# Attention and a nonlocal block on one core: reciprocals of the softmax sums kept as one row per unit, and three pieces of the last image's work moved forward

## The chip, the cores and the metric

The kernel runs on one core of a Trainium2 chip, in float32. The metric is the device time of one execution in microseconds; less is better. The work is done by the core's engines side by side: TensorE (PE) multiplies matrices, VectorE (DVE) and ScalarE (ACT) do elementwise work, GpSimd (POOL) a little of it, and SyncE (SP) issues most of the transfers (DMA) between the DRAM and the on-chip memory. Each engine works through its own instructions in the order in which they stand in its program, and waits on semaphores for the others.

## The reference

There are 8 images of 512 channels and 32 x 32 = 1024 positions. Two layers follow each other:

```python
# layer 0: attention over the positions, 8 heads of 64 channels, with a residual
q, k, v = conv1x1(x, Wq, bq), conv1x1(x, Wk, bk), conv1x1(x, Wv, bv)      # (B, 8, 64, 1024)
attn = softmax(einsum('bhdn,bhdm->bhnm', q, k) * 64**-0.5, axis=-1)
x1 = x + conv1x1(einsum('bhnm,bhdm->bhdn', attn, v), Wp, bp)
# layer 1: a nonlocal block without softmax, 256 inner channels, then a norm over the batch
g, theta, phi = conv1x1(x1, g_w, g_b), conv1x1(x1, theta_w, theta_b), conv1x1(x1, phi_w, phi_b)
f = einsum('bcn,bdn->bcd', theta, phi) / 1024
z = conv1x1(einsum('bcd,bdn->bcn', f, g), W_w, W_b) + x1
out = (z - mean(z)) * rsqrt(var(z) + 1e-5) * gamma + beta                # over images and positions
```

## The kernel before, in words

**Products.** A 1x1 convolution is a matrix product of 512 (or 256) channels with the 1024 positions. `seven` forms it from seven products of quarter blocks instead of eight (the scheme of Strassen and Winograd): VectorE forms four sums of the data's quarters (`data_sums`, `more_sums`; t1 = 12 - 11, t2 = 22 - t1, t3 = 22 - 12, t4 = 21 - t2), TensorE forms the seven products in four PSUM banks, and the results are added up in SBUF by VectorE, the first of each quarter mostly by ScalarE. In some products two of the seven are split once more (`nested`; tiles with `_in_` in their names: `pk_in_s` and so on), which needs one more VectorE addition for each small product. The order of the TensorE instructions, and of those of VectorE and SyncE that are wrapped in `dve(...)` and `sp(...)`, is kept as it is written; the others are placed by a scheduler.

**Attention of one image** (`attention`). There are 4 pairs of heads and 2 halves of the queries: 8 units `u`, each of 8 blocks of keys `m`, 64 steps in all. A step is eight TensorE instructions for the scores `ps` (L423), an exponential on ScalarE (`e`, L426), an addition on VectorE into `acc` (L432), and, two steps later, eight TensorE instructions for `po` with v (L449). `acc` of a unit is 128 key rows x 2 heads x 512 queries, to be summed over the key rows. For that, `spread` (L459) sends it by four transfers to 32 partitions of the tile `fold`, so that four units stand beneath each other: units 0 to 3 are group 0, units 4 to 7 group 1. Three VectorE additions (L478) and one product with a matrix of ones (`columns`, tile `den`, L396) finish the sums, in a form in which every unit and head has 16 equal rows. `denominators` takes the reciprocal of all 128 rows on VectorE (L486) and writes them to the DRAM (`den_d`, L488). `normalize` reads one row of each sixteen back, sent to 64 partitions each (tile `r`, L497, four transfers of 512 KB), and multiplies `o`, the attention's result, by `r` in four VectorE instructions (L503). The buffer of `r` is that of `fold`: it can only be filled when `fold` has been read.

**The order of the stages.** While image b ends its attention, the sums for image b + 1 begin, and its q, v and k products (`pq`, `pv`, `pk`) stand between the attention of image b and its projection `pp`; `denominators` comes after `pq`, the products o*r come near the end of `pv`. Then follow `pp` with Wp (which makes x1), `ptp` (theta and phi; tile `tp`), `pg` (g), `pf` (f), `pwf` (f joined to W_w) and `pz` (z). In the last image, b = 7, there is no next image to stand in between. Instead the nonlocal block of image 6 was held back: its `pf` runs inside the attention of image 7, and its `pg`, `pwf` and first `pz` stand between the attention and the projection of image 7. For it the sums of image 6's x1 are formed once more (tiles `t_x_6_again`, shown as `t_x_again`, L202), from `near_end` (L746): in the last image `near_end` is called by the last step, forms t1 and t2, then calls `spread` for the last unit (the argument `midway` of `more_sums`), then forms t3 and t4. The reciprocals of group 0 are done at step 46 there, those of group 1 between the products of `pg`:

```python
nonlocal_(b - 1, held["x"], nxt["data"], held["f"], weights("WgT"), lambda: None,
          {3: lambda: nxt.update(d=denominators(next_bank(f"den_{b}_1")[:, 0, :]))})
z[b - 1] = [held["x"][:, cc, :] for cc in range(CC)]
between = {4: late_unit(b - 1, 0)}
normalize(nxt["d"])()
```

`theta_phi` (L536) forms the sums t3 and t4 of x1 after its first product. `put_away` (L638) writes g and wf of an image to the DRAM for the end; the last stage (`last_z`) finishes z of three images and writes all eight.

Of the kernel before, what the change touches and what calls it, by code (L numbers as in the profile page):

```python
# [8 lines left out]
F32 = mybir.dt.float32  # L9
# [7 lines left out]
P = 128  # L17
# [13 lines left out]
def unshifted(ctx: ExitStack, tc: tile.TileContext, a: dict, out: bass.AP):  # L31
    nc = tc.nc
    B, C, H, W = a["x"].shape
    N = H * W
    CC = C // P
    NB = N // P
    NH = N // 512
    D = C // HEADS
# [3 lines left out]
    IC = CI // P  # L42
# [23 lines left out]
    dve = sp = pe  # L66
# [123 lines left out]
    def data_sums(quarters, name, which=(1, 2, 3, 4), **how):  # L190

        data = dict(zip(("11", "12", "21", "22"), quarters), name=name)
        more_sums(data, which, **how)
        return data

    def more_sums(data, which, pin=lambda ins: None, midway=lambda: None):
        for i in which:
            l, r = {1: ("12", "11"), 2: ("22", "t1"), 3: ("22", "12"), 4: ("21", "t2")}[i]
            if i == 3:
                midway()  # L200
            data[f"t{i}"] = block(f"t{i}_{data['name']}")
            pin(nc.vector.tensor_tensor(data[f"t{i}"], data[l], data[r], ALU.subtract))  # L202

# [11 lines left out]
    def quarters_of(t):  # L215
        return [t[:, k * CC // 2:(k + 1) * CC // 2, h * 512:(h + 1) * 512] for k in range(2) for h in range(NH)]
# [91 lines left out]
    for x_part, w_part in (((0, 1, 0), (w_first[:, 0], 0, 0, 0, 1)), ((1, 2, 0), (w_first[:, 0], 0, 0, 1, 2)),  # L308
                           ((2, 4, 0), (w_first[:, 1], 0, 1, 0, 2)), ((0, 2, 1), (w_first[:, 2], 1, 1, 0, 2)),
                           ((2, 4, 1), (corner["WqT"], 1, 0, 0, 2))):  # L310
        c0, c1, h = x_part
# [86 lines left out]
    def attention(b, q, k, v, near_end, make_f=None):  # L398

        units = [(p, h) for p in range(NPAIR) for h in range(NH)]
        steps = [(u, m) for u in range(len(units)) for m in range(NB)]
        es, accs, sums, folded, o = {}, {}, {}, {}, {}
        tags = list(free)

        def part(u):
            p, h = units[u]
            return o["o"][:, p, h * 512:(h + 1) * 512]

        def scores(i):
            u, m = steps[i]
            p, h = units[u]
            ps = bank(tags[(0, 1, 3)[i] if i < 3 else (i + 1) % 2], f"ps_{b}_{u}_{m}")
            for j in range(2):
                r = slice(j * D, (j + 1) * D)  # L420
                for c in range(2):
                    keys = slice(m * P + c * P // 2, m * P + (c + 1) * P // 2)
                    pe(nc.tensor.matmul(ps[c * P // 2:(c + 1) * P // 2, j, :], k[r, p, keys],  # L423
                                        q[r, p, h * 512:(h + 1) * 512], start=True, stop=True, skip_group_check=True))
            e = block(f"e_{b}_{u}_{m}")
            nc.scalar.activation(e, ps, AF.Exp, scale=SCALE)  # L426
            es[u, m] = e
            if m == 1:
                accs[u] = w3.tile([P, 2, 512], F32, tag="acc", name=f"acc_{b}_{u}")
                nc.vector.tensor_tensor(accs[u], es[u, 0], e, ALU.add)  # L430
            elif m > 1:
                ins = nc.vector.tensor_tensor(accs[u], accs[u], e, ALU.add)  # L432
                if i == len(steps) - 1 and not make_f:
                    dve(ins)
            if m == NB - 1 and u == len(units) - 1 and make_f:
                near_end(lambda: spread(u, dve))
            elif m == NB - 1:
                spread(u)

        def weighted(i):  # L440
            u, m = steps[i]
            p, _ = units[u]
            if m == 0:
                sums[u] = bank(tags[2 + u % 2], f"po_{b}_{u}")
            ps, e = sums[u], es.pop((u, m))
            for r in range(2):
                keys = slice(r * P // 2, (r + 1) * P // 2)
                for j in range(2):
                    pe(nc.tensor.matmul(ps[j * D:(j + 1) * D, r, :], v[keys, m, (2 * p + j) * D:(2 * p + j + 1) * D],  # L449
                                        e[keys, j, :], start=(m == 0), stop=(m == NB - 1), skip_group_check=True))  # L450
            if m == NB - 1:
                if not o:
                    o["o"] = mats.tile([P, CC, N], F32, tag="o", name=f"o_{b}")
                nc.scalar.copy(part(u), ps[:, 0, :])
                ins = nc.vector.tensor_tensor(part(u), part(u), ps[:, 1, :], ALU.add)
                if i == len(steps) - 1 and not make_f:
                    dve(ins)

        def spread(u, pin=lambda ins: None):  # L459

            g, i = divmod(u, 4)
            if i == 0:
                folded[g] = foldp.tile([P, 4, 1024], F32, tag="fold", name=f"fold_{b}_{g}")
            acc = accs.pop(u).rearrange("p j n -> p (j n)")
            for k in range(4):
                eng = nc.scalar if make_f and u == len(units) - 1 and k % 2 else nc.sync
                eng.dma_start(folded[g][i * P // 4:(i + 1) * P // 4, k, :], acc[k * P // 4:(k + 1) * P // 4, :])
            if i == 3:
                t = folded[g]
                if g == 1 and not make_f:  # L470
                    return
                if g == 0:
                    folded[g] = fold1.tile([P, 1, 1024], F32, tag="fold1", name=f"fold1_{b}")
                for part_of in fold_parts(g, t, pin):
                    part_of()

        def fold_parts(g, t, pin):
            return [lambda to=to, l=l, r=r: pin(nc.vector.tensor_tensor(to, l, r, ALU.add)) for to, l, r in (  # L478
                (t[:, 0], t[:, 0], t[:, 1]), (t[:, 2], t[:, 2], t[:, 3]), (folded[g][:, 0], t[:, 0], t[:, 2]))]

        def denominators(g, ps):

            t = folded.pop(g)
            columns(ps, folds, lambda j: t[:, 0, j * 512:(j + 1) * 512])
            ri = t[:, 0, :512]
            nc.vector.reciprocal(ri, ps)  # L486
            d = dram2.tile([P, 512], F32, tag="den", name=f"den_d_{b}_{g}")
            nc.sync.dma_start(d, ri)  # L488
            return d

        def normalize(d):

            r = foldp.tile([P, 8, 512], F32, tag="fold", name=f"r_{b}")
            for g in range(2):
                for j in range(2):
                    rows_of = d[g].rearrange("(j i s) n -> j s i n", j=2, i=4)[j, 0]
                    sp(nc.sync.dma_start(r[j * D:(j + 1) * D, 4 * g:4 * g + 4, :], rows_of.partition_broadcast(D)))  # L497

            def products():
                for h in range(NH):  # L500
                    for g in range(2):
                        at = o["o"][:, 2 * g:2 * g + 2, h * 512:(h + 1) * 512]
                        dve(nc.vector.tensor_tensor(at, at, r[:, 4 * g + h:4 * g + 4:2, :], ALU.mult))  # L503

            return products

        for i in range(len(steps) + LAG):
            if i < len(steps):
                scores(i)
            if make_f and i == 2:  # L510
                make_f(bank(tags[2], f"pf_{b - 1}"))
            if not make_f and i == len(steps) - 2:
                near_end()
            if i >= LAG:
                weighted(i - LAG)
            if make_f and i == 46:
                first_den = denominators(0, bank(tags[2], f"den_{b}_0")[:, 0, :])
        free[:] = tags
        if make_f:
            return o["o"], lambda ps: denominators(1, ps), lambda d: normalize((first_den, d)), None  # L520
        return o["o"], denominators, normalize, fold_parts(1, folded[1], dve)
# [14 lines left out]
    def theta_phi(b, w, data, between):  # L536
# [8 lines left out]
        def first(q, ps):  # L545
            ins = nc.vector.tensor_tensor(at(q), as_tp(ps), tpb[:, int(q[0]) - 1].to_broadcast([P, NB // 2, CI]),
                                          ALU.add)
            if q == "11":
# [1 line left out]

        seven(f"ptp_{b}", w, data, True, first,
              lambda q, ps: nc.vector.tensor_tensor(at(q), at(q), as_tp(ps), ALU.add),
              {0: lambda: more_sums(data, (3, 4), pin=dve), **between})
        return tp

    def make_f(b, tp, ps):
# [81 lines left out]
    def put_away(b):  # L638

        xt, g, wf = late[b]  # L640
        for d in range(IC):
            nc.sync.dma_start(spill_g[b][:, d * N:(d + 1) * N], g[d])
        nc.sync.dma_start(spill_g[b][:, IC * N:], wf)

    def take_back(b):
        t = wr.tile([P, IC * N + IC * C], F32, tag="w", name=f"gwf_{b}")
# [93 lines left out]
    for b in range(B):  # L740
# [2 lines left out]
        if not last:  # L743
            nxt["x"] = load_x(b + 1)

        def near_end(midway=None):  # L746
            if last:
                nxt["data"] = data_sums(quarters_of(held["x"]), f"x1_{b - 1}_again", pin=dve, midway=midway)
            else:
                nxt["data"] = data_sums(quarters_of(nxt["x"]), f"x_{b + 1}", (1, 2))  # L750

        def held_f(ps):
            held["f"] = make_f(b - 1, held["tp"], ps)
# [40 lines left out]
        if b == B - LATE:  # L794
            for cc in range(CC):
                nc.sync.dma_start(spill[b][:, cc, :], xt[:, cc, :])
        data = data_sums(quarters_of(xt), f"x1_{b}", (1, 2))
        if last:
            reload_chunks(B - LATE)
        elif b > B - LATE and b != B - 2:  # L800
# [241 lines left out]
```

## Time and profile before

| | |
|---|---|
| time, median of 3 runs | 2181.84 us (2181.07 to 2182.1) |
| span of the profiled execution | 2180.1 us, 29638 instructions |
| TensorE busy | 2142.0 us, 98% of the span |
| VectorE busy | 1423.3 us, 65% |
| ScalarE busy | 741.5 us, 34% |
| DMA, mean over the span | 102 GB/s |
| `pp` of image 1 to `pp` of image 2 (530.47 to 795.83 in the chain of waits) | 265.4 us |
| r, 32 transfers of 512 KB, median from issue to landing | 9.8 us |

The profile names each instruction by its line, its engine, and the tiles that it writes and reads (`out<-in`). "Busy" is the time in which an engine had work in it; the waits are the idle stretches in front of an instruction, put down to what ended them. A wait put down to "issue" is one for which the profile shows no releaser. The chain of waits follows the execution back from its last instruction; where an engine's work runs without a break, the chain stays on it.

### The profile page before, as it was taken

What the parts mean: (1) busy time and instruction counts of PE and PEld (TensorE: products, weight loads), DVE (VectorE), ACT (ScalarE), POOL (GpSimd) and SP (SyncE); (2) the same over time, 40 slices, a digit from 0 to 9 for tenths busy, and PEclk for the clock granted to TensorE, in tenths of its full rate; (3) what the DMA queues carried; (4) which work ended last, traced back from release to release, by engine and by line L of the source; (5) the groups of instructions that cost most, each with busy time, mean ns of one, the idle gap of its engine ahead of it and who ended that gap; (6) DMA issues with size and microseconds to landing.
All of it is one profiled execution on the core that took longest, in us unless ns stands there. A gap on an engine that the chain in (4) does not pass through costs nothing.

```text
span 2180.1 us, 29638 instructions
## 1 busy us (share of the span) xinstructions
PE 2142.0 (98%) x12454; PEld 1109.4 (51%) x12454; DVE 1423.3 (65%) x1612; ACT 741.5 (34%) x848; POOL 45.1 (2%) x50
## 2 busy tenths in 40 slices
PE   9999999999999999999999999999999999999896
PEld 4534663356733566336563366533665346733362
DVE  6477656776477764777747767467673777568626
ACT  1463104631046310562106621165203641065015
POOL 0000100000000000000000000000000000000000
PEclk9999999999999999999999999999999999999998
DMA  6312433124131232313323132231424115111739
GB/s 215 133 38 62 127 150 130 40 66 118 68 131 40 77 108 101 108 40 84 99 93 107 40 103 97 111 81 39 132 99 153 40 30 158 57 40 39 262 127 358
DMA packets 58893, 223.40 MB, mean 102 GB/s; under 512 B 9344, under 2 KB 15744, under 8 KB 53248
## 3 DMA queue, kind: packets, MB, share of 16 engines
q1 hardware_dynamic: 57264, 220.11, 31.8%
q8 instruction: 100, 1.64, 0.3%
q10 hardware_dynamic: 1488, 1.32, 0.2%
q14 instruction: 41, 0.34, 0.0%
HBM read 138.03 MB, written 49.81 MB: 86 GB/s over the span
## 4 chain that ended last, share of the span: by engine, by line
PE 93%; DMA 2%; DVE 2%; issue 1%; ACT 1%; SPq 0%; DVEq 0%
PE ps L423 20%; PE po L449 20%; PE ptp L276 9%; PE pp L276 7%; PE pv L276 7%; PE pq L276 6%; PE pk L276 6%; PE pg L276 4%; PE pf L561 3%; PE pz L276 2%; PE pk_in_s L239 2%; PE pq_in_s L239 2%; PE pp_in_s L239 2%; PE pz L671 2%; DMA r<-den_d 1%; PE pwf L596 1%
## 5 line engine op out<-in xcount | busy, mean ns | idle before, releaser
L426 ACT ACTIVATE e<-ps 128x1024 f32<-128x1024 f32 x512 | 522.9, 1025 | 427.9 <-PE ps L423 422.4
L432 DVE TENSOR_TENSOR acc<-acc,e 128x1024 f32<-128x1024 f32 x384 | 470.0, 1224 | 129.3 <-ACT e L426 121.6
L449 PE MATMUL po<-e,v 64*64 64x512 f32 x4096 | 528.7, 589 | 0.7 <-ACT w_WgT L563 0.7
L423 PE MATMUL ps<-q,k 64*64 64x512 f32 x4096 | 529.1, 589 | 0.0
L449 PEld LDWEIGHTS po<-e,v 64*64 64x64 f32 x4096 | 156.5, 133 | 283.4 <-issue 275.4
L423 PEld LDWEIGHTS ps<-q,k 64*64 64x64 f32 x4096 | 155.6, 133 | 284.1 <-issue 275.0
L584 ACT ACTIVATE g<-pg,gb 128x512 f32<-128x512 f32 x31 | 21.3, 687 | 398.8 <-PE pg L276 395.9
L430 DVE TENSOR_TENSOR acc<-e,e 128x1024 f32<-128x1024 f32 x64 | 78.2, 1222 | 108.7 <-ACT e L426 73.4
L276 PE MATMUL ptp<-w_tp,t_x 128*128 128x256 f32 x512 | 116.7, 384 | 2.4 <-DVE t_x L202 2.4
L276 PE MATMUL pv<-w_WvT,t_x 128*128 128x256 f32 x512 | 114.5, 379 | 0.0
L276 PEld LDWEIGHTS ptp<-w_tp,t_x 128*128 128x128 f32 x512 | 97.8, 192 | 16.1 <-DVE t_x L202 2.9
L276 PEld LDWEIGHTS pv<-w_WvT,t_x 128*128 128x128 f32 x512 | 97.2, 190 | 13.2
L276 PE MATMUL pp<-t_o,w_WpT 128*128 128x512 f32 x208 | 100.9, 592 | 0.0
L276 PE MATMUL pq<-t_x,w_WqT 128*128 128x512 f32 x200 | 98.8, 593 | 0.9 <-DVE w_WqT L723 0.9
L276 PE MATMUL pk<-t_x,w_WkT 128*128 128x512 f32 x200 | 98.9, 592 | 0.0
L379 ACT COPY v<-pv 128x1024 f32<-128x1024 f32 x32 | 32.4, 1012 | 191.2 <-PE pv L276 191.2
L276 PE MATMUL pv<-w_WvT,x 128*128 128x256 f32 x384 | 87.5, 381 | 0.0
L276 PE MATMUL ptp<-w_tp,x 128*128 128x256 f32 x384 | 86.8, 379 | 0.0
L380 DVE TENSOR_TENSOR v<-v,pv 128x1024 f32<-128x1024 f32 x24 | 29.3, 1222 | 79.9 <-PE pv L276 79.9
L276 PEld LDWEIGHTS pv<-w_WvT,x 128*128 128x128 f32 x384 | 72.4, 190 | 15.7 <-issue 5.9
L276 PEld LDWEIGHTS ptp<-w_tp,x 128*128 128x128 f32 x384 | 73.0, 190 | 13.3 <-issue 3.6
L276 PE MATMUL pp<-o,w_WpT 128*128 128x512 f32 x144 | 70.1, 611 | 7.8 <-issue 5.2
(181 smaller groups left out, 2200.4 us busy)
## 6 DMA issues: line engine op xcount, KB each, us to landing
fold<-acc SPq DMA_DIRECT2D x254, 128.0 KB, 2.3
r<-den_d SPq DMA_DIRECT2D x32, 512.0 KB, 9.8
x<-in_x_dram SPq DMA_DIRECT2D x31, 512.0 KB, 6.1
w_WqT<-kept_WqT SPq DMA_DIRECT2D x7, 2176.0 KB, 8.8
w_WkT<-kept_WkT SPq DMA_DIRECT2D x7, 2176.0 KB, 8.3
w_WpT<-kept_WpT SPq DMA_DIRECT2D x6, 2176.0 KB, 8.9
w_WvT<-kept_WvT SPq DMA_DIRECT2D x7, 1792.0 KB, 7.2
w_tp<-kept_tp SPq DMA_DIRECT2D x7, 1792.0 KB, 7.4
```

Of the source, the lines that this page charges most:

```text
L239: pe(nc.tensor.matmul(ps, a[wi], d[di], start=s not in begun, stop=True, skip_group_check=True))
L276: pe(nc.tensor.matmul(to_ps, lhsT(k), rhs(k), start=(s, at) not in begun, stop=(k == nk - 1), skip_group_check=True))
L379: seven(f"pv_{b}", w, data, True, lambda q, ps: nc.scalar.copy(at(q), as_v(ps)), lambda q, ps: dve(nc.vector.tensor_tensor(at(q), at(q), a ...
L380: lambda q, ps: dve(nc.vector.tensor_tensor(at(q), at(q), as_v(ps), ALU.add)), between)
L423: pe(nc.tensor.matmul(ps[c * P // 2:(c + 1) * P // 2, j, :], k[r, p, keys], q[r, p, h * 512:(h + 1) * 512], start=True, stop=True, skip_gr ...
L426: nc.scalar.activation(e, ps, AF.Exp, scale=SCALE)
L430: nc.vector.tensor_tensor(accs[u], es[u, 0], e, ALU.add)
L432: ins = nc.vector.tensor_tensor(accs[u], accs[u], e, ALU.add)
L449: pe(nc.tensor.matmul(ps[j * D:(j + 1) * D, r, :], v[keys, m, (2 * p + j) * D:(2 * p + j + 1) * D], e[keys, j, :], start=(m == 0), stop=(m ...
L561: pe(nc.tensor.matmul(ps[:, c, :], tp[:, i, c * P:(c + 1) * P], tp[:, i, CI:], start=(i == 0), stop=(i == NB - 1)))
L596: pe(nc.tensor.matmul(ps, f[:, c, d * P:(d + 1) * P], ww[:, c, :], start=(c == 0), stop=(c == IC - 1)))
L671: pe(nc.tensor.matmul(ps[:, h - h0, :], wf[:, d, oc * P:(oc + 1) * P], g[d][:, h * 512:(h + 1) * 512], start=(d == 0), stop=(d == IC - 1), ...
```

## The change

What the change does, in the order of the diff:

- The reciprocals are written as one row for each unit and head: 8 rows of 512 (16 KB) in place of 128 rows (256 KB). `rows_of` then reads the four rows of one group and head as one run of 8 KB for each of 64 partitions, where before it was four runs of 2 KB.
- In the last image, the reciprocal of group 1 goes to a small tile of its own (`ri`), so that `fold` is free, and `r` can be filled, as soon as the product `den` has read it. The rows of group 0 are then loaded at once, ahead of group 1's reciprocal.
- The products o*r are done group by group instead of half by half.
- In the last image, `near_end` is called three times: t1 of image 6's x1 after step 59, t2 after step 61, and t3 and t4 at the end, after the last unit's transfers have been issued and ahead of the additions of the folding.
- `theta_phi` finds t3 and t4 of x1 done in the last image, ahead of its first product.
- The writes of image 6's g and wf are kept in their written order on SyncE, behind the loads of r.

```diff
-    def more_sums(data, which, pin=lambda ins: None, midway=lambda: None):
+    def more_sums(data, which, pin=lambda ins: None):
         for i in which:
             l, r = {1: ("12", "11"), 2: ("22", "t1"), 3: ("22", "12"), 4: ("21", "t2")}[i]
-            if i == 3:
-                midway()
...
             if m == NB - 1 and u == len(units) - 1 and make_f:
-                near_end(lambda: spread(u, dve))
+                spread(u, dve, near_end)
...
-        def spread(u, pin=lambda ins: None):
+        def spread(u, pin=lambda ins: None, meanwhile=lambda: None):
...
             if i == 3:
                 t = folded[g]
+                meanwhile()
                 if g == 1 and not make_f:
                     return
...
-            ri = t[:, 0, :512]
+            alone = make_f and g == 1
+            ri = (fold1.tile([P, 1, 1024], F32, tag="fold1", name=f"ri_{b}") if alone else t)[:, 0, :512]
             nc.vector.reciprocal(ri, ps)
-            d = dram2.tile([P, 512], F32, tag="den", name=f"den_d_{b}_{g}")
-            nc.sync.dma_start(d, ri)
+            if alone:
+                rows_of(0, first_den)
+            d = dram2.tile([8, 512], F32, tag=f"den{g}", name=f"den_d_{b}_{g}")
+            nc.sync.dma_start(d, ri.rearrange("(a s) n -> a s n", a=8)[:, 0, :])
             return d
 
+        def rows_of(g, d):
+            if "all" not in rows:
+                rows["all"] = foldp.tile([P, 8, 512], F32, tag="fold", name=f"r_{b}")
+            rows[g] = rows["all"][:, 4 * g:4 * g + 4, :].rearrange("q i n -> q (i n)")
+            for j in range(2):
+                sp(nc.sync.dma_start(rows[g][j * D:(j + 1) * D, :],
+                                     d.rearrange("(j i) n -> j (i n)", j=2)[j].partition_broadcast(D)))
+
         def normalize(d):
-            r = foldp.tile([P, 8, 512], F32, tag="fold", name=f"r_{b}")
             for g in range(2):
-                for j in range(2):
-                    rows_of = d[g].rearrange("(j i s) n -> j s i n", j=2, i=4)[j, 0]
-                    sp(nc.sync.dma_start(r[j * D:(j + 1) * D, 4 * g:4 * g + 4, :], rows_of.partition_broadcast(D)))
+                if g not in rows:
+                    rows_of(g, d[g])
+            r = rows["all"]
 
             def products():
-                for h in range(NH):
-                    for g in range(2):
+                for g in range(2):
+                    for h in range(NH):
                         at = o["o"][:, 2 * g:2 * g + 2, h * 512:(h + 1) * 512]
                         dve(nc.vector.tensor_tensor(at, at, r[:, 4 * g + h:4 * g + 4:2, :], ALU.mult))
...
-            if not make_f and i == len(steps) - 2:
+            if i in ((len(steps) - 5, len(steps) - 3) if make_f else (len(steps) - 2,)):
                 near_end()
...
-              {0: lambda: more_sums(data, (3, 4), pin=dve), **between})
+              {0: lambda: "t3" in data or more_sums(data, (3, 4), pin=dve), **between})
...
+        spill_dma = sp if b == B - 2 else lambda ins: None
         for d in range(IC):
-            nc.sync.dma_start(spill_g[b][:, d * N:(d + 1) * N], g[d])
-        nc.sync.dma_start(spill_g[b][:, IC * N:], wf)
+            spill_dma(nc.sync.dma_start(spill_g[b][:, d * N:(d + 1) * N], g[d]))
+        spill_dma(nc.sync.dma_start(spill_g[b][:, IC * N:], wf))
...
-        def near_end(midway=None):
-            if last:
-                nxt["data"] = data_sums(quarters_of(held["x"]), f"x1_{b - 1}_again", pin=dve, midway=midway)
+        def near_end():
+            if not last:
+                nxt["data"] = data_sums(quarters_of(nxt["x"]), f"x_{b + 1}", (1, 2))
+            elif "data" not in nxt:
+                nxt["data"] = data_sums(quarters_of(held["x"]), f"x1_{b - 1}_again", (1,))
+            elif "t2" not in nxt["data"]:
+                more_sums(nxt["data"], (2,))
             else:
-                nxt["data"] = data_sums(quarters_of(nxt["x"]), f"x_{b + 1}", (1, 2))
+                more_sums(nxt["data"], (3, 4), dve)
...
-        data = data_sums(quarters_of(xt), f"x1_{b}", (1, 2))
+        data = data_sums(quarters_of(xt), f"x1_{b}", (1, 2, 3, 4) if last else (1, 2))
```

More of the change, by code (lines that the diff above doesn't have):

```diff
@@ L408, in attention @@
         es, accs, sums, folded, o = {}, {}, {}, {}, {}
+        rows = {}
         tags = list(free)
```

## The prediction

> **What bounds the kernel now.** I read the page's busy shares first, then TensorE's waits, then the timeline around each wait.
>
> ```profile
> PE 2142.0 (98%) x12454; PEld 1109.4 (51%) x12454; DVE 1423.3 (65%) x1612; ACT 741.5 (34%) x848; POOL 45.1 (2%) x50
> ...
> PE pp L276 <- issue: 5.2, 1, 5.2
> PE pk_in_s L239 <- DVE k L298: 3.0, 2, 2.2
> PE pp L276 <- DVE o L503: 2.6, 1, 2.6
> PE ptp L276 <- DVE t_x L202: 2.4, 1, 2.4
> ```
>
> TensorE is the bound: 98% busy, and the change leaves its instructions and their order untouched. So only its waits can be won or added. Four kinds lie inside the work; the change touches all four. The first, third and fourth are in the last image:
>
> ```profile
> 2028.35 0.33 SPq L488 DMA_DIRECT2D den_d<-fold  x1
> 2030.60 3.75 SPq L497 DMA_DIRECT2D r<-den_d  x4
> 2032.46 3.60 PE L671 MATMUL pz<-g,wf 128*128 128x512 f32 x8
> 2039.91 1.23 DVE L503 TENSOR_TENSOR o<-o,r 128x1024 f32<-128x1024 f32 x1 [9.00 <-DMA r<-den_d]
> 2041.24 5.88 PE L276 MATMUL pp<-o,w_WpT 128*128 128x512 f32 x8 [5.18 <-issue]
> 2047.16 1.41 DVE L530 SCALAR_TENSOR_TENSOR x<-pp,bp,x 128x512 f32<-128x512 f32 x2 [6.02 <-PE pp L276]
> 2048.49 3.49 DVE L503 TENSOR_TENSOR o<-o,r 128x1024 f32<-128x1024 f32 x3
> 2049.76 3.70 PE L276 MATMUL pp<-o,w_WpT 128*128 128x512 f32 x8 [2.63 <-DVE o L503]
> ...
> 2085.61 1.22 DVE L202 TENSOR_TENSOR t_x<-x 128x1024 f32<-128x1024 f32 x1
> 2086.75 1.22 DVE L202 TENSOR_TENSOR t_x<-x,t_x 128x1024 f32<-128x1024 f32 x1
> 2086.89 5.27 PE L276 MATMUL ptp<-w_tp,t_x 128*128 128x256 f32 x16 [2.45 <-DVE t_x L202]
> 2092.00 3.62 PE L276 MATMUL ptp<-w_tp,x 128*128 128x256 f32 x16
> ```
>
> The wait called "issue" is really one for r: TensorE stops at 2036.06, the first product o*r runs as soon as r lands (2039.91), and pp follows. The eight pp matmuls then take 5.88 us where eight take 3.60 elsewhere. So r costs 5.18 idle and 2.28 of slow matmuls. The next 2.63 us has another cause: VectorE's second product stands behind two sums that read pp. The ptp wait is for t_x 3, which VectorE reaches late: 2.45 idle and 5.27 - 3.62 = 1.65 slow.
>
> The second kind is in images 0 and 3; here image 3, and the queue's traffic while only r moves (1031 to 1037 us) and while only the stored images move (2052 to 2070 us): packets, MB, share of 16 engines.
>
> ```profile
> 1025.94 3.76 SPq L497 DMA_DIRECT2D r<-den_d  x4
> 1043.10 3.50 DVE L503 TENSOR_TENSOR o<-o,r 128x1024 f32<-128x1024 f32 x3 [6.24 <-DMA r<-den_d]
> 1046.99 0.70 PE L239 MATMUL pk_in_s<-i_x,w_WkT 128*128 128x256 f32 x2 [2.19 <-DVE k L298]
> ...
> q1 hardware_dynamic: 494, 0.96, 100.8%
> ...
> q1 hardware_dynamic: 1959, 7.13, 101.8%
> ```
>
> r has landed 17.2 us after its first issue (1043.10 - 1025.94); VectorE, in order, holds the k sums behind it, and TensorE runs out of banks. In the chain of waits, first to last pk matmul is 21.81 us in image 1 (506.94 to 528.75), 24.65 in image 3, 23.30 in image 0: 2.84 + 1.49 = 4.33 us lost. In image 1, r lands 2.5 us after pk began and nothing is lost; image 0: 4.0, image 3: 5.3.
>
> **What the Trainium skill says.** "DMA: Bandwidth & Descriptors", section on why small descriptors are slow: a packet carries a fixed cost, so longer runs move more. The trace agrees only in part: r's packets of 2 KB take 6 x 1.008 x 16 / 494 = 196 ns each, and those of the stored images, 3.6 KB, take 18 x 1.018 x 16 / 1959 = 150 ns. So r pays something besides size; all of it re-reads the same few rows. The same page, section on the anatomy of one DMA: about 2 us are fixed, mostly the receipt of the write. The trace has 1.99 (image 0) and 2.97 us (image 3) for den_d. Same page, section on the semaphore's 16: a slowest dimension of 8 uses 8 engines; for the 16 KB that is no cost I can see, and no run here shows it. "TensorE: Matmul & The Clock Gate", Part 1: after an idle window of about 3.4 us the clock halves. The trace agrees for the 5.18 us gap (weight loads 0.86 us apart instead of 0.43), but it also slowed after 2.45 and not after 2.63.
>
> **The change part by part.**
>
> (a) *Last image, group 0 of r early.* Its two loads wait only for the fold tile, whose last reader is the den matmul. That starts at 2022.29 and takes 1.08, so they issue near 2023.4, into an idle queue (0 packets from 2023 to 2028). Even at r's present rate, 0.96 MB in 6 us, the 1 MB takes 6.6 us plus 2 fixed: landed by 2032. On SyncE nothing is behind these loads that could go sooner: den_d needs the reciprocal. VectorE's own work in front of the product ends at about 2030.9, as it does now. Product: 1.2. So pp can start when pz ends: 2036.06. Saved: 5.18 + 2.28 = 7.46. The products now run group by group, so pp needs only group 0 here.
>
> (b) *Group 1.* With the sums t_x_again no longer between folds and reciprocal, the reciprocal starts when den is out, near 2023.4 instead of 2024.97, and ends near 2026.8. den_d (16 KB, 8 rows) lands after 2.0 to 3.0, or a little later if it queues behind group 0: 2029 to 2031.5. Then 1 MB more: 2034 to 2040. It is wanted when the two sums on pp are done: 2039.5 + 1.4 = 2040.9. In the compiled order of VectorE's instructions the new kernel still has those sums in front of group 1's products, so the 2.63 us wait stays. I count nothing.
>
> (c) *t1, t2 inside the attention loop.* Two subtractions of 1.22 us. VectorE idles 0.49 in each step of 1.72 there; each backlog of about 0.7 is gone two steps later, before the last acc. t3, t4 fill the 2.4 us between the last acc (2014.55) and the fold (2017.97), which waits for its DMA. Cost: nothing. The 0.21 wait of pwf goes: 0.2.
>
> (d) *x1 sums t3, t4 before the tp sums.* On VectorE they move to about 2073.2 to 2075.5 (old time); the first tp sum shifts from 2074.11 to 2075.4 and ends at 2076.7. Who waits for it: the third ptp product reuses that bank, at 2077.36. Hidden, by 0.7. Saved: 2.45 + 1.65 = 4.10.
>
> (e) *Images 0 to 6, 8 KB rows and short den_d.* No view shows an 8 KB broadcast, so I bound it. Slow end: r keeps its rate; then only the shorter den_d (2.97 to about 2 us in image 3) and the first t_o sum, now done before the wait instead of between two k sums behind it (some 0.3 in each of the two images), count: about 1.5. Fast end: r moves like the stored images, 2 MB in 5 us instead of 12.7, and lands before pk starts; all 4.33 go. It needs only 2.8 us of r's 17 for that, so I take 4.33.
>
> (f) *Held-back spills behind the load of w_tp.* Nothing on the path waits for them; w_tp is issued after pwf as now.
>
> Sum: 7.46 + 0.2 + 4.10 + 4.33 = 16.1. 2181.84 - 16.1 = 2165.7.
>
> **Rivals.**
>
> *r keeps its rate.* For: packets of r are slow beyond their size; if the cause is the re-reading, one 8 KB row may not cure it. Against: four pieces become one run. Gain 7.7 + 4.1 + 1.5 = 13.3: 2168.5. Chance 0.2.
>
> *A remainder in the last image.* The 2.63 gap now falls in a different phase of the clock and halves it (1.7, as after the ptp gap), or group 1 lands up to 2 us after 2040.9. Speaking for it: the 2.45 us gap did slow the clock; w_tp follows r in the queue. Against: 2.63 did not. About 2 to 4 us back: 2169. Chance 0.12.
>
> *The remainder goes too.* If VectorE reaches group 1 before pp is out, 2.6 more: 2163.1. The compiled order speaks against it. Chance 0.04.
>
> *Slower.* If 16 engines on one 8 KB stretch are slower, r lands later in seven images, and image 1 shows no slack beyond about 0.5 us. A quarter slower is 15.2 to 19 us: 3.4 x 7 = 24 lost, 11.8 won: 2194. Against: same bytes, fewer descriptors. Chance 0.06, some 2 more for what I can't see.
>
> **How the numbers follow.** The forecast, 2165.7, has 0.56. The range runs from 2162.5 (with the remainder gone) to 2171.0 (slow r and part of a remainder together). The bounds of 0.2% are 2177.5 and 2186.2: faster 0.90, same 0.03, slower 0.07.
>
> **What would show it.** In the profile after: r from issue to landing clearly below 9.8 us median; no pk_in_s wait; pp of image 7 starting when pz ends, in some 3.6 us per eight; a wait of about 2.6 before its second group; no wait of ptp for t_x. Wrong if VectorE waits longer for r in images 1, 2, 4 to 6, if ptp waits for a tp sum, or if acc of the last steps slips.

## The result, and the profile after

The changed kernel takes 2165.37 us (median of 6, 2164.1 to 2166.24), the kernel before 2182.16 us beside it: 0.9923 of it, 95% interval 0.991 to 0.9935. The forecast was 2165.7. The six times lie in two kinds, 2164.1 to 2164.73 and 2166.01 to 2166.24, three of each; the median falls between them, where no execution was.

The page's busy shares and TensorE's waits of the changed kernel, in the order in which they were read before (engine, line, what was waited for; us in total, times, longest):

```profile
PE 2137.3 (99%) x12454; PEld 1110.0 (51%) x12454; DVE 1427.6 (66%) x1612; ACT 740.9 (34%) x848; POOL 43.2 (2%) x50
...
PE pp L274 <- DVE o L513: 2.6, 1, 2.6
PE warm_ps L316 <- DVE warm L302: 1.1, 1, 1.1
PE pq L274 <- DVE w_WqT L734: 0.7, 1, 0.7
PE po L448 <- ACT w_WgT L573: 0.7, 1, 0.7
PE den L394 <- PE pg L274: 0.5, 1, 0.5
```

Of the four waits of before, three are gone: the 5.2 us in pp, those of pk_in_s, and that of ptp. The 2.6 us between the first two groups of pp are still there. The timeline of the last image (start, length, engine, line):

```profile
2018.25 1.11 SPq L499 DMA_DIRECT2D r<-den_d  x2
2018.25 3.36 DVE L487 RECIPROCAL ri<-den 128x512 f32<-128x512 f32 x1 [0.62 <-PE den L394]
2021.64 0.60 SPq L491 DMA_DIRECT2D den_d<-ri  x1
2025.15 1.10 SPq L499 DMA_DIRECT2D r<-den_d  x2
2025.19 2.36 DVE L513 TENSOR_TENSOR o<-o,r 128x1024 f32<-128x1024 f32 x2 [0.90 <-DMA r<-den_d]
2026.83 3.60 PE L682 MATMUL pz<-g,wf 128*128 128x512 f32 x8
2030.27 3.60 PE L274 MATMUL pp<-o,w_WpT 128*128 128x512 f32 x8
2033.90 1.41 DVE L540 SCALAR_TENSOR_TENSOR x<-pp,bp,x 128x512 f32<-128x512 f32 x2 [5.09 <-PE pp L274]
2035.23 2.35 DVE L513 TENSOR_TENSOR o<-o,r 128x1024 f32<-128x1024 f32 x2
2036.50 5.40 PE L274 MATMUL pp<-o,w_WpT 128*128 128x512 f32 x8 [2.63 <-DVE o L513]
```

Group 0 of r is loaded as soon as den is out, its products end at 2027.5, and pp starts where pz ends, in 3.60 us for its eight. Then VectorE does the two sums on pp before it reaches group 1's products, as forecast. But the eight matmuls behind that wait now take 5.40 us in the profiled execution, which is one of the slower kind; before, behind the same wait, they took 3.70. And in images 0 to 6, here image 3:

```profile
1022.91 2.41 SPq L499 DMA_DIRECT2D r<-den_d  x4
1033.83 2.35 DVE L513 TENSOR_TENSOR o<-o,r 128x1024 f32<-128x1024 f32 x2
1037.36 2.35 DVE L513 TENSOR_TENSOR o<-o,r 128x1024 f32<-128x1024 f32 x2
```

In none of these images does a product wait for r. The four loads are issued in 2.41 us instead of 3.76.

Where the 15.9 us between the two profiled executions (2180.1 and 2164.2) came from, by the starts in the two chains of waits:

| stretch | before | after | won | forecast |
|---|---|---|---|---|
| start to pp of image 6 (1847.94, 1842.78) | 1847.94 | 1842.78 | 5.16 | 4.33 |
| to the first pz of the last image (2032.62, 2027.00) | 184.68 | 184.22 | 0.46 | 0.2 |
| to ptp of the last image (2070.62, 2059.06) | 38.00 | 32.06 | 5.94 | 7.46 |
| to the end (2180.1, 2164.2) | 109.48 | 105.14 | 4.34 | 4.10 |

The 5.16 us are 1.65 in image 0 and 3.00 in image 3, from one start of pk to the next, and some 0.5 spread over the others.

### The profile page after: what moved, and what is told of

It is laid out like the page before. It is cut to its first block, busy times and chain, and to the rows that moved or that the text cites. A ratio compares the mean times of both kernels' runs of the same rounds, so it can differ in the third digit from the quotient of the medians.

```text
span 2164.2 us, 29633 instructions
## 1 busy us (share of the span) xinstructions
PE 2137.3 (99%) x12454; PEld 1110.0 (51%) x12454; DVE 1427.6 (66%) x1612; ACT 740.9 (34%) x848; POOL 43.2 (2%) x50
## 4 chain that ended last, share of the span: by engine, by line
PE 98%; DVE 1%; ACT 1%; DMA 0%; issue 0%
PE ps L422 20%; PE po L448 20%; PE pv L274 9%; PE ptp L274 9%; PE pp L274 7%; PE pk L274 7%; PE pq L274 6%; PE pg L274 4%; PE pf L571 3%; PE pz L274 2%; PE pk_in_s L237 2%; PE pq_in_s L237 2%; PE pp_in_s L237 2%; PE pz L682 2%; PE pwf L606 1%; PE den L394 1%
## 5 line engine op out<-in xcount | busy, mean ns | idle before, releaser
L478 DVE TENSOR_TENSOR fold<-fold 128x1024 f32<-128x1024 f32 x48 | 58.7, 1222 | 26.0 <-DMA fold<-acc 25.5
```

## The experiments

Each ratio is to the kernel before, measured beside the run. The runs lie in three groups, measured apart: experiments 1, 2 and 5 and the first run of 8; then 6, 7, the first run of 3 and the run of 8 with late sums; then 4, the second run of 3, and in 8 the changed kernel once more and the second run. The kernel before itself differs by up to 2 us between groups, so small differences are read within a group or from the trace.

**1. The rows alone.** In the kernel before:

```diff
-            d = dram2.tile([P, 512], F32, tag="den", name=f"den_d_{b}_{g}")
-            nc.sync.dma_start(d, ri)
+            d = dram2.tile([8, 512], F32, tag=f"den{g}", name=f"den_d_{b}_{g}")
+            nc.sync.dma_start(d, ri.rearrange("(a s) n -> a s n", a=8)[:, 0, :])
...
-                    rows_of = d[g].rearrange("(j i s) n -> j s i n", j=2, i=4)[j, 0]
-                    sp(nc.sync.dma_start(r[j * D:(j + 1) * D, 4 * g:4 * g + 4, :], rows_of.partition_broadcast(D)))
+                    rows_of = d[g].rearrange("(j i) n -> j (i n)", j=2)[j]
+                    to = r[:, 4 * g:4 * g + 4, :].rearrange("q i n -> q (i n)")
+                    sp(nc.sync.dma_start(to[j * D:(j + 1) * D, :], rows_of.partition_broadcast(D)))
```

> The kernel before with one edit: 8 rows written to den_d, read back as runs of 8 KB; the order of all VectorE instructions is that of before. Theory (the 8 KB runs alone let r land in time in images 0 to 6): the 4.3 to 5.2 us of pk are won, and in the last image r lands 1 to 2 us sooner: 5.5 to 7 us faster than before, some 2175.5. Rival (the new order of the products o*r and t_o is what frees the k sums): under 2 us faster.

Measured: 2172.44 us, 0.9951 (0.9937 to 0.9964): 10.2 us faster, more than expected. TensorE's waits that concern it, and the last image:

```profile
PE pp L276 <- issue: 3.8, 1, 3.8
PE pp L276 <- DVE o L504: 2.6, 1, 2.6
PE ptp L276 <- DVE t_x L202: 2.4, 1, 2.4
...
2035.04 5.27 PE L276 MATMUL pp<-o,w_WpT 128*128 128x512 f32 x8 [3.85 <-issue]
2042.95 3.70 PE L276 MATMUL pp<-o,w_WpT 128*128 128x512 f32 x8 [2.63 <-DVE o L504]
...
2080.08 3.72 PE L276 MATMUL ptp<-w_tp,t_x 128*128 128x256 f32 x16 [2.45 <-DVE t_x L202]
```

The pk_in_s waits are gone with the old order of VectorE's work, so the new order of products and t_o sums isn't needed for that. The profiled executions differ by 8.4 us. Of these, 5.2 lie between pk of image 0 and pp of image 6 (1604.30 us here). Of the rest, 1.3 us is the shorter wait in pp, 0.6 the matmuls behind it (5.27, before 5.88), and 1.5 the matmuls behind the wait of ptp: 3.72 here, 5.27 before, after the same 2.45 us. So some 2 us are matmuls that happened to run at full speed; the last section says when they do.

**2. Rows near each other, but runs of 2 KB.** In the changed kernel:

```diff
-            d = dram2.tile([8, 512], F32, tag=f"den{g}", name=f"den_d_{b}_{g}")
+            d = dram2.tile([8, 1024], F32, tag=f"den{g}", name=f"den_d_{b}_{g}")[:, :512]
...
-            rows[g] = rows["all"][:, 4 * g:4 * g + 4, :].rearrange("q i n -> q (i n)")
+            rows[g] = rows["all"][:, 4 * g:4 * g + 4, :]
...
-                sp(nc.sync.dma_start(rows[g][j * D:(j + 1) * D, :],
-                                     d.rearrange("(j i) n -> j (i n)", j=2)[j].partition_broadcast(D)))
+                sp(nc.sync.dma_start(rows[g][j * D:(j + 1) * D, :, :],
+                                     d.rearrange("(j i) n -> j i n", j=2)[j].partition_broadcast(D)))
```

> The changed kernel, with the 8 rows of den_d 4 KB apart in the DRAM, so that r is read in runs of 2 KB again; write of 16 KB and all orders kept. Theory (length of run sets r's rate): 196 ns per 2 KB again, pk_in_s waits again in images 0 and 3 or more, 3 to 5 us slower than the changed kernel (2168.5 to 2170.5). Rival (the short write, the closer rows or the order of the products did it): within 1.5 us of the changed kernel.

Measured: 2165.89 us, 0.9921 (0.9907 to 0.9935); the changed kernel had 0.9923. The theory fell: no pk_in_s waits, and from pk of image 0 to pp of image 6 it takes 1604.29 us, as in the changed kernel (1604.31).

**3. Rows far apart.** The same with `[8, 8192]`, which puts the rows 32 KB apart, as before; run twice:

> The changed kernel, with the 8 rows of den_d 32 KB apart in the DRAM, as the rows that the kernel before read were, in runs of 2 KB; the write stays 16 KB. Theory (the distance of the rows sets r's rate): some 196 ns per packet of 2 KB, against 148 with rows 4 KB apart; r lands 3 us later, and pk_in_s waits in some images: 2 to 5 us slower than the changed kernel. Rival (the write of 256 KB before it is what slowed r): 150 ns per packet, within 1 us of the changed kernel.

> Rows 32 KB apart, once more. Theory (distance of the rows sets r's rate): slower than the changed kernel by 2 to 3 us. Rival (the difference before was between chips): within 1 us of it.

Measured: 2168.20 us, 0.9944 (0.993 to 0.9957), and 2167.94 us, 0.9944 (0.9931 to 0.9958), the latter 3.4 us behind the changed kernel in its group (2164.53). The queue's traffic from 494 to 499 us, while only r moves, first for the changed kernel, then for rows 4 KB apart, then for rows 32 KB apart (packets, MB, share of 16 engines):

```profile
q1 hardware_dynamic: 174, 1.16, 101.2%
```

```profile
q1 hardware_dynamic: 566, 1.10, 104.5%
```

```profile
q1 hardware_dynamic: 443, 0.87, 82.5%
```

Over 5 us these are 232, 220 and 174 GB/s: the run's length gives 5%, the rows' distance 21%. Counted from the issue of r, ten us bring 1.92 to 2.04 MB in images 1 and 3 of six traces with runs of 8 KB, 1.83 and 1.84 with rows 4 KB apart, and 1.50 to 1.53 with rows 32 KB apart (both runs), so both steps stand clear of the spread. A packet of 2 KB takes 148 ns near (5 x 1.045 x 16 / 566) and 149 far; in image 3 it is 150 near and 112 to 139 far. So the packets are not slower; the engines have fewer of them in work. The issue shows it too: four loads take 2.41, 2.66 and 3.56 us. The loss of rows far apart is not where it was expected, though. From pk of image 0 to pp of image 6 both runs take 1604.29 to 1604.49 us, as the changed kernel does. It is in the last image, here of the second run:

```profile
2037.19 6.63 PE L274 MATMUL pp<-o,w_WpT 128*128 128x512 f32 x8 [3.67 <-DVE o L513]
```

Group 1 of r comes after the two sums, the wait is 1.0 longer, and the matmuls behind it take 6.63 us, where the changed kernel had 5.40 or 3.70. In the first run the wait is 0.9 longer and they take 5.19.

**4. The short write alone.** In the kernel before, only the eight rows that are read are written, to their old places:

```diff
-            nc.sync.dma_start(d, ri)
+            nc.sync.dma_start(d.rearrange("(a s) n -> a s n", a=8)[:, 0, :], ri.rearrange("(a s) n -> a s n", a=8)[:, 0, :])
```

> The kernel before with one edit: only the 8 rows that are read are written, to the places 32 KB apart that they had (16 KB instead of 256); read in runs of 2 KB as before. Theory (the rows' distance is the cause): r keeps some 170 GB/s, and at most 2 us of the 10 that the near rows gave the same kernel. Rival (the size of the write is the cause): 8 to 10 us faster than before.

Measured: 2177.74 us, 0.9985 (0.9979 to 0.9992): 3.3 us faster, between the two. In the trace it is 4.2 us from pk of image 0 to pp of image 6: 1605.28, against 1609.5 before (1847.94 - 238.43; the 238.43 is the start in the timeline, 238.27, and the 0.16 by which the chain lags it) and 1604.30 with the rows near (experiment 1). The first 5 us after r's issue in image 3, in the kernel before and then here:

```profile
q1 hardware_dynamic: 244, 0.49, 34.8%
```

```profile
q1 hardware_dynamic: 321, 0.63, 41.2%
```

In image 1 the kernel before moves 0.63 MB in these 5 us, as it does here. So behind the write of 256 KB, r starts badly in image 3, which lost most. There the loads are also issued 3.10 us behind den_d, with the short write 1.91, and the last product waits until 17.2 us after their issue, with the short write 15.0. How the write slows the reads behind it, no run here shows.

**5. The sums of x1 late.** In the changed kernel:

```diff
-        data = data_sums(quarters_of(xt), f"x1_{b}", (1, 2, 3, 4) if last else (1, 2))
+        data = data_sums(quarters_of(xt), f"x1_{b}", (1, 2))
```

> The changed kernel, with t3 and t4 of x1 back after the tp sums. Theory: ptp waits 2.45 us for t_x again and runs 1.65 slow: 4.1 us slower than the changed kernel (2169.5). Rival (what is won there is given back at the end by transfers): 0 to 1 us slower.

Measured: 2168.66 us, 0.9933 (0.9919 to 0.9946). The wait is back, without slow matmuls behind it:

```profile
2075.22 3.72 PE L274 MATMUL ptp<-w_tp,t_x 128*128 128x256 f32 x16 [2.45 <-DVE t_x L200]
```

Nothing is given back at the end: this profiled execution is 2.8 us longer than that of the changed kernel (2167.0, 2164.2), with the same 5.40 us in pp. The sums' place is worth 2.45 us for sure, and the 1.65 us of slow matmuls only where they occur.

**6. No early load of group 0** (the one line `alone = False`), and **7. the sums t_x_again late again**, each in the changed kernel; of the second, cut:

```diff
-                spread(u, dve, near_end)
+                near_end(lambda: spread(u, dve))
...
+                nxt["data"] = data_sums(quarters_of(held["x"]), f"x1_{b - 1}_again", (1, 2), pin=dve)
+                midway()
                 more_sums(nxt["data"], (3, 4), dve)
```

> The changed kernel, with the reciprocal of group 1 left in the fold tile, so that all four loads of r in the last image follow den_d. Theory (the early load of group 0 is what lets pp start when pz ends): group 0 then lands some 7 us after 2025, its product ends at 2033 to 2034 where pz ends at 2030.3: 2.5 to 4 us idle and up to 2.3 slow; with the later wait of 2.63 no longer followed by slow matmuls, 3 to 5 us slower than the changed kernel (2168.4 to 2170.4). Rival (r is fast enough now to come in time anyway): under 1 us.

> The changed kernel, with the four sums t_x_again after the last step of the attention again, t3 and t4 behind the folding. Theory (their place only delays group 1's reciprocal, by some 1.6 us, and group 1 is awaited behind the two sums on pp anyway): 0 to 0.5 us slower than the changed kernel. Rival (the reciprocal is on the path): 1.6 us slower or more.

Measured: 2168.26 us, 0.9945 (0.9931 to 0.9958), and 2165.43 us, 0.9933 (0.9919 to 0.9946). Without the early load pp waits, but less than expected:

```profile
2023.35 2.41 SPq L499 DMA_DIRECT2D r<-den_d  x4
2030.65 2.36 DVE L513 TENSOR_TENSOR o<-o,r 128x1024 f32<-128x1024 f32 x2 [6.59 <-DMA r<-den_d]
2031.98 3.67 PE L274 MATMUL pp<-o,w_WpT 128*128 128x512 f32 x8 [1.78 <-issue]
```

Group 0 comes 7.3 us after the issue, where it took 9.3 before, and the issue stands 6.85 us ahead of pz's end, 5.46 before: 1.1 of that from the reciprocal and 0.3 from the shorter write. So without the early load the old wait of 5.18 is down to 1.78. The place of the sums t_x_again shows no difference in the times. In the trace it does: from den to pz it is 10.17 us, and 9.69 in the changed kernel, the 0.21 of wait in front of pwf among it.

**8. All four products first.** In the changed kernel the two sums on the first pp product are kept behind the products on VectorE:

```diff
-                nc.vector.scalar_tensor_tensor(at, ps[:, m, :], bp[:, c:c + 1], at, ALU.add, ALU.add)
+                ins = nc.vector.scalar_tensor_tensor(at, ps[:, m, :], bp[:, c:c + 1], at, ALU.add, ALU.add)
+                if b == B - 1 and q == "11":
+                    dve(ins)
```

> The changed kernel, with the two sums on the first pp product of the last image kept behind all four products o*r on VectorE. Theory (those two sums alone hold group 1's product, and the wait alone slows the matmuls after it): the wait of 2.63 us and the 1.8 us of slow matmuls go, 4.3 us faster than the changed kernel (2161.1). Rival (group 1 of r lands only just in time): 0 to 2 us faster, with the wait put down to r.

> The kernel with all four products first, and with the sums t_x_again late as in the run before. Theory: there group 1 of r is awaited by TensorE itself (0.28 us of wait), so the reciprocal's 1.6 us show: 1.3 to 2 us slower than the kernel with all products first (2163.4 to 2164.1), and more if the matmuls behind the wait slow down. Rival: no difference.

> The changed kernel once more, beside the next three on the same chip: 0.992 of the kernel before. Its times should fall into two groups some 1.7 us apart, by whether the wait of 2.63 us in pp halves TensorE's clock or not.

> All four products first, once more: if the 2.63 us wait and what follows it are all that differs, 2.4 us faster than the faster group of the changed kernel's times and 4.1 faster than the slower group, and in one group only.

Measured: 2162.06 us, 0.9905 (0.989 to 0.9921), and again 2161.49 us, 0.9914 (0.9899 to 0.9929), beside 2164.53 us, 0.9931 (0.9918 to 0.9945), of the changed kernel. It is the fastest kernel of the study. Its pp:

```profile
2029.94 3.60 PE L274 MATMUL pp<-o,w_WpT 128*128 128x512 f32 x8
2032.54 2.36 DVE L513 TENSOR_TENSOR o<-o,r 128x1024 f32<-128x1024 f32 x2 [3.50 <-DMA r<-den_d]
2033.82 3.70 PE L274 MATMUL pp<-o,w_WpT 128*128 128x512 f32 x8 [0.28 <-DVE o L513]
```

The times of the changed kernel in this last group fall in two again: 2164.26, 2164.37, 2164.53 with a granted clock of 0.996, and 2166.09, 2166.20 with 0.995. Its profiled execution there, of the first kind, has 3.70 us behind the wait where the earlier one had 5.40:

```profile
2036.40 3.70 PE L274 MATMUL pp<-o,w_WpT 128*128 128x512 f32 x8 [2.63 <-DVE o L513]
```

With all products first there is one kind only: 2161.23 to 2161.86, 2.9 below the first kind and 4.7 below the second (middle to middle).

With the sums late as well: 2162.31 us, 0.9918 (0.9905 to 0.9932). It was measured in another group, so the times alone don't settle it. The trace does, and the theory fell: the reciprocal is 1.6 us later there, and TensorE does not wait for group 1 at all; the profiled execution is 0.6 and 0.9 us longer than the two with early sums, most of it the 0.5 between den and pz. The queue explains it. With the sums early, den_d is issued at 2021.64 and the loads behind it at 2025.15, 3.5 us later; with the sums late the two stand at

```profile
2023.47 0.60 SPq L491 DMA_DIRECT2D den_d<-ri  x1
2025.93 1.11 SPq L499 DMA_DIRECT2D r<-den_d  x2
```

2.5 us apart. In experiment 6, with no load of group 0 ahead of den_d, they are 1.9 apart; in experiment 3, where group 0 is read more slowly, 4.9. So an earlier den_d lands only with the traffic of group 0's loads, and the reciprocal's gain is lost there.

## Why the prediction was right, by its own steps

**(a), the early group 0 and the end of pp's wait: right, with a term left out.** The idle 5.18 and the slow 2.28 us are gone. The step let group 0 land by 2032 of the old time scale; it landed 6.9 us after its issue, and its products were done 2.7 us before pz was. The stretch still won 5.94 and not 7.46: the matmuls behind the remaining 2.63 us wait took 1.8 more in the profiled execution. That was the rival "a remainder in the last image", right in its mechanism, put at 1.7 us and, with what else it held, at a chance of 0.12. The runs show that it comes and goes within one kernel, so the chance was too low: three of six times in the result, two of five in the last group. The rule in the last section puts it near 0.6. And the early load is worth 1.8 us of the wait; the faster r (2.0) and its earlier issue (1.4) were worth the other 3.4.

**(b), the 2.63 us wait stays: right**, and for the stated cause; taking the two sums out of the way removed it (experiment 8).

**(c), t_x_again costs nothing: right.** The last acc was not late. It brings 0.46 us where 0.2 was forecast: the 0.21 of pwf, and some more beside it (experiment 7).

**(d), the x1 sums: right in kind.** The wait of 2.45 us went. The 1.65 us of slow matmuls were counted as a cost of the wait, but they are a matter of the execution: experiments 1, 4 and 5 have the wait without them.

**(e), the images 0 to 6: right in size (5.16 for 4.33), wrong in cause.** The step took the run of 8 KB as what brings r in time, and gave the shorter write "about 1.5" if r kept its rate. Experiment 2 takes the long runs away and loses nothing between pk of image 0 and pp of image 6. Experiment 4 changes only the write, and wins 4.2 us of the 5.2, with r still slow (1.52 MB in its first ten us; before, 1.47 in image 1 and 1.29 in image 3). The last 1.0 came with near rows read as one run in the old order of VectorE's work (experiment 1); in the new order rows far apart cost none of it (experiment 3). No run has the new order with the long write. The error did not show in the sum, because either cause ends the same waits. The step also took the 196 ns of a packet as a price of re-reading the rows. With the same rows and the short write, a packet takes 124 ns from 5 to 10 us after the issue in image 3 (461 packets, 71.3%), in the kernel before 194 (416, 100.7%): the long packets go with the long write. "DMA: Bandwidth & Descriptors", on small descriptors, holds here as a difference of 5% between runs of 2 and 8 KB, and this was read as if it could cure more. The fixed part was the better hint, not by the page's 2 us, which its section on the anatomy of one DMA gives for transfers that GpSimd issues (these are SyncE's), but by the 1.99 to 2.97 us of den_d in the kernel before: the write is in the line of waits.

**(f): right**; nothing waits for the spills.

In the profiled executions the errors of (a), -1.5, of (e), +0.8, and of (c) and the end, +0.5, leave 15.9 for the 16.1 of the sum. That 2165.7 and 2165.37 are so near is luck beyond that: the wrong cause in (e) did no harm to the sum, and the median fell between two kinds of execution.

## What to carry to other kernels

Of a small tensor that makes a round trip through the DRAM, write only what is read; that won most in the images 0 to 6. Put it close together too: rows far apart were read at 0.8 of the rate and cost some 1 us of wait in the last image. The length of the runs changed no wait that TensorE had. When a wait is removed, look at what stands next on the in-order engine behind it: here two sums, which could be done later, kept 2.6 us. An earlier producer gains nothing where its transfer stands in a queue behind a larger one that was put ahead of it.

## What the runs showed of the hardware that was not expected

- A pause of 2.45 to 2.63 us of TensorE slows the matmuls behind it in some executions (5.27, 5.40, 6.77 us for groups that take 3.6) and not in others of the same kernel (3.70), and the traces show when. In all 14, the record of the granted clock changes only at points that lie whole multiples of 3.413 us apart, from 1.00 to 0.50 or back; the grid of points lies differently in each execution. Two pieces of this grid in the changed kernel's profile of the result, two in its profile in the last group, then three in experiment 2 (piece, length, busy PE, PEld, DVE, ACT, POOL, granted clock, share and GB/s of DMA):

```profile
2033.23:2036.65 3.42, 0.79 (x3) 0.15 (x2) 2.75 (x4) 0.00 (x0) 0.00 (x0) 1.00 0.93 389
2036.65:2040.06 3.41, 3.41 (x5) 1.35 (x6) 3.38 (x4) 0.00 (x0) 0.00 (x0) 0.50 1.04 380
```

```profile
2032.11:2035.52 3.41, 1.66 (x4) 0.38 (x2) 1.71 (x3) 0.00 (x0) 0.00 (x0) 1.00 1.05 446
2035.52:2038.94 3.42, 2.54 (x6) 1.25 (x7) 3.39 (x4) 0.00 (x0) 0.00 (x0) 1.00 0.95 389
```

```profile
2032.39:2035.81 3.42, 1.40 (x4) 0.33 (x2) 1.99 (x3) 0.00 (x0) 0.00 (x0) 1.00 1.04 440
2035.81:2039.22 3.41, 2.80 (x4) 1.25 (x5) 3.38 (x4) 0.00 (x0) 0.00 (x0) 0.50 0.96 390
2039.22:2042.63 3.41, 3.41 (x6) 1.35 (x5) 1.81 (x2) 0.00 (x0) 0.00 (x0) 0.50 1.01 366
```

  The same pause of 2.63 us lies whole in one piece in the first and is cut in two, 1.75 and 0.88, in the second. Over all pieces of the 14 traces: at full clock, the 26 with 2.02 us or more without a matmul are followed by half clock, and the other 8749, with up to 1.98, are not, without exception; at half clock, the 12 with up to 0.58 are followed by full clock, and the 4 with 0.61 or more by half clock again. So a pause under 2 us cost no clock here (1.78: 3.67), and a longer one does if at least 2 us of it fall into one piece. As an estimate from these numbers, if the grid lies anyhow, that is (3.41 + 2.63 - 2 x 2.0) / 3.41 = 0.6 for the 2.63 us; one piece at half clock loses 3.41 / 2 = 1.7. "TensorE: Matmul & The Clock Gate", Part 1, puts the window at 3.4 us and calls it free-running; both agree. It lets the clock fall after an idle window; here 2.02 us of one was enough.
- 64 partitions reading the same four rows of 2 KB: 174 GB/s with the rows 32 KB apart and 220 with 4 KB, at packets of 149 and 148 ns; and 232 as one run of 8 KB. Stored images, each byte read once, moved at 397 GB/s. So neither change of layout comes near the rate of a plain load. That the re-reading is what costs the rest is likely, but no run here reads rows of the same size without it.
